# Multi-query attention, 64 sequences on one core: value products in the key-block order 0, 3, 1, 2, and the four bias heads of a partition as neighbours

## The chip, the core and the metric

The kernel runs on one core of a Trainium2 chip. A core has five engines that run their own instruction streams: TensorE (PE in the profile; PEld is its weight load), VectorE (DVE), ScalarE (ACT), GpSimd (POOL) and SyncE (SP). Here SP issues nearly all DMA transfers, one after the other, and 16 DMA engines carry them. The metric is device time in microseconds (us), the median of several executions. One more execution is taken with the hardware profiler; the profile and the trace come from it.

## The reference, cut to what matters

```python
# x: 64 x 128 x 512; 16 heads of 64, one shared key/value head; f32 throughout
xn = layernorm(x, g_in)
q = (xn @ Wq).reshape(b, n, 16, 64).transpose(0, 2, 1, 3) * 64 ** -0.5
k, v = split(xn @ Wkv)                        # 64 columns each
k, v = [null_k; k], [null_v; v]               # one null key and value in front
sim = einsum('bhid,bjd->bhij', q, k) + [null_attn_bias, attn_bias]
sim = where(causal or masked, -max, sim)
out = einsum('bhij,bjd->bhid', softmax(sim), v)
out = out.transpose(0, 2, 1, 3).reshape(b, n, 1024) @ Wo
return x + layernorm(out, g_out)
```

`attn_bias` is 16 x 128 x 128. It is the same for all 64 batches (sequences), so the kernel loads it once.

## The kernel before

**Tiles.** A batch is 128 tokens. Its scores lie in one tile `S[b]` of 128 partitions: a partition holds one query row of a quarter of the heads. The 128 partitions are four groups ("quads") of Q = 32, and a quad holds the same 32 query places for NE = 4 heads. Query rows are cut in four blocks of 32, and since the attention is causal, block i needs only its first (i + 1) x 32 keys. So a partition's row holds for each of its four heads the four blocks with 32, 64, 96 and 128 keys behind each other (`BLOCK[i]`), and a null column beside each. The blocks 0 and 1 are the first half (`KEYS[0]`, 192 columns of two heads in a PSUM room), 2 and 3 the second.

**Heads.** The four heads of a partition are stored in the order (r, f): r is the half of a 128-column query block in which a head lies, f the block. A head is number 8v + 4u + 2f + r, where 2u + v is the quad. Since r is the outer index in the tile and the inner one in the head's number, `load_bias` (lines 197 to 206) makes one transfer for each u, block, v and r: 32 in all, of 32 x 2 rows each. A row has 32, 64, 96 or 128 columns of f32.

**Bias, once, at the start.** `load_second` queues on SP: the input tiles `x_4` to `x_7`, a small key load, the bias of u = 1, `nbh` (the null bias), the bias of u = 0. Behind them on SP, in this order, come the key copies of `kv_pair_out` (line 397), the mask of the first four batches (`load_mask`, line 141), the value round trip (`vd`, `vr`, lines 407 and 412), `nv2`, `x_8` and `x_9`, the second mask, and then `wo` and `gob`. A transfer's completion semaphore is one of eight that go round, so a transfer also waits until the one eight before it has landed. GpSimd cuts the loaded bias to the causal triangle (`causal`, line 214), VectorE takes the null bias off (`null_shift`, lines 230 and 235), and then `bias_add` (line 684, GpSimd) adds bias and mask into `S[b]` for each batch. The mask goes through ScalarE first (`mask_neg`, line 671, tile `mneg`). On ScalarE, `mask_neg(0)` stands in front of the copies of two query blocks (line 460) that the first scores need.

**Loop.** Two batches a, b are one turn (`turn`, `body`; the last two are written out in `turn_end`, `body_end`). A turn's scores are computed on TensorE in 64 x 64 tiles (line 731), added into `S` by VectorE (`scores_add`, lines 746 and 748), reduced to a maximum, put through exp on ScalarE (line 767), scaled on GpSimd (line 791), and transposed in 32 x 32 blocks by VectorE into `sb` (line 821). In the next turn's head, behind that turn's scores, `values` multiplies them with the values. Then comes TensorE's work for the next group's queries (lines 367, 516, 582, 648) and for the output projection (line 953). Every engine takes its instructions in the order written; the order is set by hand.

**Value products.** `values(b)` (lines 860 to 881) runs over the key blocks j = 0 to 3. Key block j is seen by the query blocks i = j to 3, so its product has (4 - j) x 32 query columns for each of two heads: 256, 192, 128 and 64 columns. Each j is one wave of 8 matmuls on 8 array tiles (four quads s in the rows, two head halves r in the columns), each with its own weights, 32 values x 64. Wave j = 0 writes all of the PSUM room, the others add to the part they see. A matmul in f32 shows in the trace as two passes, each with its own weight load.

Of the kernel before, what the change touches and what calls it, by code (L numbers as in the profile page):

```python
# [17 lines left out]
def kernel(  # L18
# [59 lines left out]
    nc = tc.nc  # L78
    B, N, DIM = x.shape
    H = attn_bias.shape[0]  # L80
    DH = w_kv.shape[1] // 2
# [8 lines left out]
    Q = 32  # L90
    NQ = P // Q
    NF = NC // 2
    R8 = 2 * NF
    NE = H // NQ
    NF2 = NF // 2
    KEYS_OF = tuple((i + 1) * Q for i in range(NQ))
# [3 lines left out]
    BLOCK = tuple(slice(K_AT[i], K_AT[i] + KEYS_OF[i]) for i in range(NQ))  # L100
    KEYS = slice(1, LOW - 1), slice(LOW + 1, ROW - 1)
# [49 lines left out]
    nbp = const.tile([P, NE], FP, name="nbp")  # L151
    nv2 = const.tile([P, 1], FP, name="nv2")
    nbh = const.tile([P, H], FP, name="nbh")
    biasp = const.tile([P, NE, ROW], FP, name="biasp")
# [26 lines left out]
    def load_second():  # L181
        for m in range(4, 8):
            load_x(m)
        nc.sync.dma_start(
            out=nkv, in_=cond[0:2].rearrange("r d -> (r d)").unsqueeze(1)
        )
        load_bias(1)
        nc.sync.dma_start(out=nbh, in_=null_bias.partition_broadcast(P))
        load_bias(0)
# [5 lines left out]
            )  # L195

    def load_bias(u):
        bias_r = attn_bias.rearrange("(v u f r) i j -> u v r i f j", v=2, u=2, r=2)[u]
        for i in (3, 2, 1, 0):
            for v in range(2):  # L200
                quad = slice((2 * u + v) * Q, (2 * u + v + 1) * Q)
                for r in range(2):
                    nc.sync.dma_start(  # L203
                        out=biasp[quad, r * NF2 : (r + 1) * NF2, BLOCK[i]],
                        in_=bias_r[v, r, i * Q : (i + 1) * Q, :, 0 : KEYS_OF[i]],
                    )

    def causal(u):

# [13 lines left out]

    def null_shift(u):

        rows = slice(u * DH, (u + 1) * DH)
        for v in range(2):
            quad = slice((2 * u + v) * Q, (2 * u + v + 1) * Q)
            first = v * R8 + u * NE
            nc.vector.tensor_copy(  # L230
                nbp[quad].rearrange("p (r f) -> p r f", r=2),
                nbh[quad, first : first + NE].rearrange("p (f r) -> p r f", r=2),
            )
        for keys in KEYS:
            nc.vector.tensor_tensor(
                biasp[rows, :, keys],
                biasp[rows, :, keys],
                nbp[rows].unsqueeze(2).broadcast_to([DH, NE, keys.stop - keys.start]),
                ALU.subtract,
            )  # L240
# [425 lines left out]
    S, nmax, rsum = {}, {}, {}  # L666
# [72 lines left out]
    pss = {}  # L739

    def scores_add(b, hf):
        sv = S[b][:, :, KEYS[hf]].rearrange("p (r f) j -> p r f j", r=2)
        pv = pss.pop((b, hf))
        if isinstance(pv, list):
            for r in (1, 0):
                nc.vector.tensor_tensor(sv[:, r], pv[r], sv[:, r], ALU.add)
        else:
            nc.vector.tensor_tensor(sv, pv, sv, ALU.add)
# [111 lines left out]
    def values(b):  # L860

        g, t = divmod(b, GB)
        sb = sbs.pop(b)
        for j in range(NQ):
            slots = slice(j * (1 + SLOT), j + SLOT * SLOT + 1, SLOT)
            for s in range(NQ):
                quad = slice(s * Q, (s + 1) * Q)
                for r in range(2):
                    nc.tensor.matmul(  # L869
                        pos[b][s][r * DH : (r + 1) * DH, :, j * Q :].rearrange(  # L870
                            "p f (i q) -> p f i q", q=Q
                        ),
                        vr[g][quad, t, j, :],
                        sb[quad, slots, r * NF2 : (r + 1) * NF2, :].rearrange(
                            "p i f q -> p f i q"
                        ),
                        start=(j == 0),
                        stop=True,
                        skip_group_check=(j > 0),
                        tile_position=(s * Q, r * DH),  # L880
                    )
# [159 lines left out]
    def turn(d):  # L1041

        a, b, p = 2 * d, 2 * d + 1, 2 * d - 2
        g = d // 2 + 1
        homes = (ps_y, "Y"), (ps_q, "a")
        if d == 1:
            homes = homes[::-1]
        scores(a, 0, (homes[0], (ps_w, "w")))
        scores(b, 0, (homes[1], (ps_w, "w")))
        scores(a, 1)  # L1050
        scores(b, 1, ((ps_y, "X"), (ps_q, "c")))
        scores_add(a, 0)
        scores_add(b, 0)
        scores_max(a, 0)
        scores_add(a, 1)
        scores_add(b, 1)
        po = values_rooms(p)
        values(p)
        values(p + 1)
        if d % 2 and (d + 1) // 2 < NG:  # L1060
            mask_neg((d + 1) // 2)
        bias_add(a + 2)
        if d % 2 == 0:
            token_sum(g, 1)
            token_sum(g, 2)
        exps(a, 0)
        values_out(p, po)

    def turn_end(d):

        a, b, p = 2 * d, 2 * d + 1, 2 * d - 2
        if d == PAIRS:
            blocks_T(late_T.pop(), (4,))
            late_nmr(p - 3)
            late_norm(p - 3)
            late_gain(p - 4)
            late_residual(p - 4, nc.gpsimd)
            values_rooms_apart(p)
            result_room(p)
            for m in (p, p + 1):  # L1080
                values(m)
                values_out_one(m)
            return
# [538 lines left out]
    norm_apply(6)  # L1622
    norm_T(4)
    null_shift(1)
    causal(0)
    q_batches((5,))
# [3 lines left out]
    q_batches((6,))  # L1630
    norm_T(6)
    null_shift(0)
    bias_add(0, (slice(0, LOW), slice(LOW, ROW)))
    q_half(7, 0)
# [105 lines left out]
```

## Time and profile before

| | us |
|---|---|
| median of 3 executions | 1033.31 |
| lowest, highest | 1033.29, 1035.83 |
| the profiled execution | 1035.0 |
| its span, first to last instruction | 1033.2 |
| TensorE busy in it | 1016.9 |

The mean granted clock of TensorE over the span is 0.995 of full speed. In the profile a row of a timeline or of the chain begins with its start and its length in us; "L203" is line 203 of the kernel; `x16` is a count; `[6.01 <-ACT qT L460]` is the time that the engine stood idle before, and what ended it. A row of a group ends with its busy time, the mean length of one in ns, and the idle time before. SPq, ACTq and PEq stand for what an engine's sequencer does, issuing transfers above all. Lengths of matmuls are modelled by the profiler, and a matmul's record lasts beyond its last column, so that matmuls behind each other overlap.

### The profile page before, as it was taken

The page shows a single profiled execution, that of the slowest core. Times are in us where ns is not written, and L with a number is a line of the kernel's source. Part 1 is how long each engine was busy: PE and PEld are TensorE (multiplying, and loading weights), DVE is VectorE, ACT ScalarE, POOL GpSimd, SP SyncE. Part 2 cuts the span into 40 slices and gives each one's busy share as a digit, 9 for nine tenths or more (in the row PEclk, how much of TensorE's full clock was granted, in tenths as well). Part 3 has the DMA queues.
Part 4 walks back from the last instruction along what each step waited for, and adds up shares of the span by engine and source line. Part 5 has one row for each costly group of instructions (what it writes and reads, how often), then busy time and mean ns, then how long its engine had stood idle before and what let it go on. Part 6 is the DMA issues. An engine that isn't in the chain of part 4 may idle for free.

```text
span 1033.2 us, 32182 instructions
## 1 busy us (share of the span) xinstructions
PE 1016.9 (98%) x12493; PEld 903.5 (87%) x12493; DVE 809.8 (78%) x2216; ACT 666.1 (64%) x2705; POOL 736.1 (71%) x768
## 2 busy tenths in 40 slices
PE   9799999999999999999999999999999999999997
PEld 9688888888888888888888888888888888888886
DVE  6476777787888788888787887787888787877687
ACT  4565786656766566775656866567765657755583
POOL 3687758677696676868668596776867768586676
PEclk9899999999999999999999999999999999999999
DMA  6504214152240524314142250513315142131221
GB/s 194 151 27 125 95 68 122 58 149 85 97 125 32 157 71 133 107 47 136 60 148 92 78 137 33 168 66 114 115 38 153 63 146 94 68 101 36 67 84 63
DMA packets 68017, 100.79 MB, mean 98 GB/s; under 512 B 24852, under 2 KB 30232, under 8 KB 66072
## 3 DMA queue, kind: packets, MB, share of 16 engines
q1 hardware_dynamic: 67568, 98.34, 30.8%
q8 instruction: 98, 1.61, 0.6%
q14 instruction: 55, 0.45, 0.1%
q10 hardware_dynamic: 296, 0.40, 0.1%
HBM read 63.06 MB, written 33.55 MB: 94 GB/s over the span
## 4 chain that ended last, share of the span: by engine, by line
PE 95%; DMA 2%; SPq 1%; POOL 1%; issue 1%; ACT 0%; POOLq 0%; DVE 0%; DVEq 0%
PE pyX L953 19%; PE pa L516 15%; PE pyY L953 10%; PE pc L516 10%; PE po L869 8%; PE pkv L367 6%; PE pyw L953 5%; PE pl L582 4%; PE pm L648 4%; PE ps L731 3%; PE sc_X L731 2%; PE sc_Y L731 2%; PE pq L451 1%; PE py_s L953 1%; PE sc_a L731 1%; SPq L203 1%
## 5 line engine op out<-in xcount | busy, mean ns | idle before, releaser
L767 ACT ACTIVATE s<-s,nmax 128x33 f32<-128x33 f32 (+3 forms) x1024 | 357.9, 354 | 30.5 <-DVE nmax L754 30.5
L791 POOL TENSOR_TENSOR s<-s,rinv 128x128 f32<-128x128 f32 (+3 forms) x256 | 181.7, 732 | 117.8 <-DVE rinv L785 117.7
L684 POOL TENSOR_TENSOR s<-biasp,mneg 128x1296 f32<-128x1296 f32 (+1 forms) x65 | 188.3, 2899 | 85.9 <-ACT mneg L671 58.5
L767 ACT ACTIVATION_READ_ACCUMULATOR s<-s,nmax 128x1 f32 x1024 | 196.1, 191 | 0.0
L981 ACT COPY y<-pyX 128x256 f32<-128x256 f32 x29 | 10.8, 372 | 167.8 <-PE pyX L953 155.2
L754 DVE TENSOR_REDUCE nmax<-s 128x4 f32<-128x132 f32 (+3 forms) x256 | 112.5, 482 | 0.1
L953 PE MATMUL pyX<-wT,oT 128*128 128x256 f32 x464 | 109.7, 379 | 0.0
L953 PE MATMUL pyX<-wo,oT 128*128 128x256 f32 x464 | 109.7, 379 | 0.0
L821 DVE STREAM_TRANSPOSE sb<-s 128x256 f32<-128x256 f32 (+3 forms) x194 | 103.9, 587 | 0.6 <-POOL s L791 0.5
L953 PEld LDWEIGHTS pyX<-wo,oT 128*128 128x128 f32 x464 | 86.0, 190 | 10.5
L528 ACT COPY ku<-pa 128x256 f32<-128x256 f32 x118 | 43.3, 367 | 76.5 <-issue 58.0
L869 PE MATMUL po<-sb,vr 32*64 32x256 f32 (+1 forms) x4064 | 90.3, 304 | 2.1 <-issue 2.0
L953 PEld LDWEIGHTS pyX<-wT,oT 128*128 128x128 f32 x464 | 84.0, 190 | 9.2
L869 PEld LDWEIGHTS po<-sb,vr 32*64 32x64 f32 x4064 | 79.5, 130 | 14.1 <-issue 11.5
L537 DVE TENSOR_TENSOR qT<-pc,ku 128x256 f32<-128x256 f32 x118 | 48.8, 413 | 49.4 <-ACT ku L528 25.1
L892 ACT ACTIVATE oT<-po,nv 128x512 f32<-128x512 f32 (+1 forms) x127 | 74.6, 669 | 19.4 <-PE po L869 19.4
L933 POOL TENSOR_TENSOR oT<-oT 128x512 f32<-128x512 f32 x64 | 80.6, 1277 | 4.5 <-PE pyw L953 2.2
L288 POOL TENSOR_TENSOR rstd<-rstd,nhalf 128x1 f32<-128x1 f32 x64 | 35.2, 556 | 57.5 <-DVE rstd L287 52.8
L516 PE MATMUL pa<-xS,wq 128*128 128x256 f32 x264 | 67.8, 379 | 0.0
L598 DVE TENSOR_TENSOR qT<-pl,kp 128x128 f32<-128x128 f32 x112 | 32.1, 286 | 42.7 <-PE pl L582 41.7
L367 PE MATMUL pkv<-xT,wkv 128*128 128x256 f32 x256 | 63.3, 391 | 0.4 <-issue 0.4
L516 PE MATMUL pa<-xT,wq 128*128 128x256 f32 x236 | 60.6, 379 | 0.0
(208 smaller groups left out, 2555.9 us busy)
## 6 DMA issues: line engine op xcount, KB each, us to landing
res<-in_x_dram SPq DMA_DIRECT2D x64, 256.0 KB
out_dram<-y SPq DMA_DIRECT2D x63, 256.0 KB
x<-in_x_dram SPq DMA_DIRECT2D x62, 256.0 KB
xd<-xb SPq DMA_DIRECT2D x14, 1024.0 KB
xT<-xd SPq DMA_DIRECT2D x56, 256.0 KB
vr<-vd SPq DMA_DIRECT2D x64, 128.0 KB
kT<-kT SPq DMA_DIRECT2D x32, 64.0 KB
vd<-vb SPq DMA_DIRECT2D x32, 64.0 KB
```

The source lines that it names most:

```text
L367: nc.tensor.matmul(pkv, wkv[:, kc, :], xT[g][:, t : t + 2, kc, :], start=(kc == 0), stop=(kc == KC - 1),)
L516: nc.tensor.matmul(prod[tag], w[:, kc, f * P : (f + 1) * P], t[:, :, kc, :], start=(start and kc == 0), stop=(kc == HK - 1), skip_group_ch ...
L684: nc.gpsimd.tensor_tensor(S[b][:, :, keys], biasp[:, :, keys], mneg[:, t, keys] .unsqueeze(1) .broadcast_to([P, NE, keys.stop - keys.start ...
L731: nc.tensor.matmul(home[r][u * DH : (u + 1) * DH, f, keys], qT[g, u * NF2 + f, t // 2][rows, t % 2, i], kT[rows, t, 0 : KEYS_OF[i]], start ...
L754: nc.vector.tensor_reduce(nmax[b][:, hf, k * NE : (k + 1) * NE], S[b][:, :, WITH_NULL[i]], AX.X, ALU.max, negate=True,)
L767: nc.scalar.activation(row, row, AF.Exp, bias=nmax[b][:, hf, k : k + 1], accum_out=rsum[b][:, hf, k : k + 1],)
L791: nc.gpsimd.tensor_tensor(sv, sv, rinvs[b, hf][:, k : k + NE] .unsqueeze(2) .broadcast_to([P, NE, KEYS_OF[i]]), ALU.mult,)
L821: nc.vector.transpose(sbs[b][:, at : at + n].rearrange("p j e q -> p e j q"), S[b][:, :, keys].rearrange("p e (j k) -> p e j k", k=Q),)
L869: nc.tensor.matmul(pos[b][s][r * DH : (r + 1) * DH, :, j * Q :].rearrange("p f (i q) -> p f i q", q=Q), vr[g][quad, t, j, :], sb[quad, slo ...
L892: nc.scalar.activation(to, src, AF.Identity, bias=nv2)
L933: eng.tensor_tensor(o, a, b, op)
L953: nc.tensor.matmul(prod[key], h[:, c, :], w[:, c, :], start=(start and c == 0), stop=(c == HC - 1), skip_group_check=not start,)
```

## The change

The four heads of a partition are stored in the order of their numbers, e = 2f + r. `load_bias` then takes the four neighbours in one transfer: 16 transfers of 32 x 4 rows, in the same order of u, block and v. Three places follow: the null bias is copied without a reordering; `scores_add` reads `S` with r inside f; a value product takes every second head of `sb` (`r::2`) instead of two neighbours. Apart from that, `values` takes its key blocks in the order 0, 3, 1, 2, so the waves have 256, 64, 192 and 128 columns.

```diff
     def load_bias(u):
-        bias_r = attn_bias.rearrange("(v u f r) i j -> u v r i f j", v=2, u=2, r=2)[u]
+        bias_r = attn_bias.rearrange("(v u e) i j -> u v i e j", v=2, u=2)[u]
         for i in (3, 2, 1, 0):
             for v in range(2):
                 quad = slice((2 * u + v) * Q, (2 * u + v + 1) * Q)
-                for r in range(2):
-                    nc.sync.dma_start(
-                        out=biasp[quad, r * NF2 : (r + 1) * NF2, BLOCK[i]],
-                        in_=bias_r[v, r, i * Q : (i + 1) * Q, :, 0 : KEYS_OF[i]],
-                    )
+                nc.sync.dma_start(
+                    out=biasp[quad, :, BLOCK[i]],
+                    in_=bias_r[v, i * Q : (i + 1) * Q, :, 0 : KEYS_OF[i]],
+                )
...
     def null_shift(u):
...
-            nc.vector.tensor_copy(
-                nbp[quad].rearrange("p (r f) -> p r f", r=2),
-                nbh[quad, first : first + NE].rearrange("p (f r) -> p r f", r=2),
-            )
+            nc.vector.tensor_copy(nbp[quad], nbh[quad, first : first + NE])
...
     def scores_add(b, hf):
-        sv = S[b][:, :, KEYS[hf]].rearrange("p (r f) j -> p r f j", r=2)
+        sv = S[b][:, :, KEYS[hf]].rearrange("p (f r) j -> p r f j", r=2)
...
     def values(b):
...
-        for j in range(NQ):
+        for j in (0, 3, 1, 2):
...
-                        sb[quad, slots, r * NF2 : (r + 1) * NF2, :].rearrange(
+                        sb[quad, slots, r::2, :].rearrange(
```

More of the change, by code (lines that the diff above doesn't have):

```diff
@@ L224, in null_shift @@
     def null_shift(u):
-        rows = slice(u * DH, (u + 1) * DH)
         for v in range(2):
@@ L229, in null_shift @@
             first = v * R8 + u * NE
-            nc.vector.tensor_copy(
-                nbp[quad].rearrange("p (r f) -> p r f", r=2),
-                nbh[quad, first : first + NE].rearrange("p (f r) -> p r f", r=2),
-            )
+            nc.vector.tensor_copy(nbp[quad], nbh[quad, first : first + NE])
+        rows = slice(u * DH, (u + 1) * DH)
         for keys in KEYS:
```

## The prediction

> **What bounds the kernel now.** I read the page first: busy time by engine, then the chain of waits.
>
> ```profile
> span 1033.2 us, 32182 instructions
> PE 1016.9 (98%) x12493; PEld 903.5 (87%) x12493; DVE 809.8 (78%) x2216; ACT 666.1 (64%) x2705; POOL 736.1 (71%) x768
> PE 95%; DMA 2%; SPq 1%; POOL 1%; issue 1%; ACT 0%; POOLq 0%; DVE 0%; DVEq 0%
> ```
>
> TensorE is busy for 98% and is 95% of the chain: in the loop nothing else sets the pace. An edit on another engine is worth something only where TensorE stands still; an edit to TensorE's own work counts once per turn of the loop. The change has one of each kind. So the second view was the table of stretches with the granted clock (PEclk), to see where TensorE stands still.
>
> ```profile
> 29.50:36.00 6.50, 0.49 (x5) 0.38 (x4) 1.70 (x2) 2.48 (x6) 3.96 (x10) 0.81 0.38 85
> 36.00:44.70 8.70, 8.64 (x143) 7.12 (x142) 4.32 (x10) 5.34 (x27) 8.39 (x6) 0.75 0.52 140
> 72.00:1027.00 955.00, 951.90 (x11907) 845.39 (x11895) 762.21 (x2105) 629.06 (x2584) 692.11 (x710) 1.00 0.31 95
> ```
>
> (Columns after the stretch: its length, then busy time of PE, PEld, DVE, ACT and POOL, then clock, DMA share, GB/s.) Of the 16.3 us without a matmul, 6.0 lie in one hole, from 29.5 to 36 us, and right behind it the clock is below 1: 0.81 and 0.75 in these two stretches, 1.00 in the loop. The chain of waits, in order of time, says what the hole waits for.
>
> ```profile
> 16.45 0.89 SPq L203
> ...
> 28.66 0.42 SPq L203
> 29.19 0.54 SPq L397
> 29.83 0.53 SPq L397
> 30.41 3.09 DMA m<-in_mask_BxS_bk_dram
> 33.52 1.92 ACT mneg L671 x4
> 35.44 0.25 ACT qT L460
> ```
>
> SP issues bias transfers back to back (L203), then two key copies (L397), then the mask (L141). The mask lands 3.1 us after its issue; ScalarE makes `mneg` of it (L671), and queued behind that on ScalarE is the copy of a query block (L460) for which the first scores wait. The hole is SP's issue time, passed on through the mask.
>
> The third view is the timeline of one clean turn's value products (L869), which are TensorE's own work.
>
> ```profile
> 385.11 2.62 PE L869 MATMUL po<-sb,vr 32*64 32x256 f32 x128
> 387.67 0.70 PE L367 MATMUL pkv<-xT,wkv 128*128 128x256 f32 x2
> 390.74 1.73 PE pyX L953 x8
> PEld po L869 <- issue: 11.5, 46, 0.8
> ```
>
> Two batches are 128 matmuls (64 value products of two passes each, since a product in f32 shows as two), and the next work starts 387.67 - 385.11 = 2.56 us after them. Eight array tiles work side by side, so each streams 2 x 2 x (256 + 192 + 128 + 64) = 2560 columns; at 1.73/8 = 0.216 us for 256 columns (last-but-one row, from the chain) that is 2.16 us. So 0.40 us of a clean turn is not streaming. The last row says that in some turns the weight loads also wait for nothing the profile shows, 11.5 us in all; that goes on, since the number of TensorE instructions stays.
>
> **The change part by part.**
>
> *Sixteen bias transfers instead of 32.* Bytes, row lengths and rows stay; a transfer now has 32 x 4 = 128 rows instead of 64. What it takes SP to issue:
>
> ```profile
> 1.18 1.84 SPq L164 DMA_DIRECT2D wq<-in_L_cond_Wq_dram  x4
> 4.80 0.43 SPq L178 DMA_DIRECT2D wkv<-in_L_cond_Wkv_dram  x1
> 9.18 11.91 SPq L203 DMA_DIRECT2D biasp<-in_fside_16xSxS_dram  x16
> 21.14 0.43 SPq L188 DMA_DIRECT2D nbh<-cond_null_attn_bias_dram  x1
> 21.61 7.48 SPq L203 DMA_DIRECT2D biasp<-in_fside_16xSxS_dram  x16
> ```
>
> The second group of 16 takes 7.48/16 = 0.47 us each. Four weight transfers of 128 rows of 2 KB take 1.84/4 = 0.46 each, and one of 512 rows 0.43: the price is per transfer, not per row, and I take 0.47. The first eight of the first group are stretched by waits for earlier loads (11.91 us for 16); they stay where they are, the eighth issued at 16.45 and done at 17.34, but they now hold all of the first half of the bias. Then `nbh` goes out at 17.4 instead of 21.1, the second eight run from 17.9 to 21.6 instead of 21.6 to 29.1: 7.5 us earlier. Everything behind them on SP moves with them: both key copies, the mask, `vd`, `vr`, `nv2`, `x_8`, `x_9`, the second mask, `wo`, `gob`.
>
> The key copies need the keys, and the hole has neighbours:
>
> ```profile
> 20.98 0.47 ACT L391 ACTIVATE kT<-pkv,nkv 64x256 f32<-64x256 f32 x1
> 25.70 0.57 ACT L321 COPY xT<-pxT 128x512 f32<-128x512 f32 x1
> 28.91 0.60 PE L320 MATMUL pxT<-wR,x 128*128 128x128 f32 x4
> 35.75 0.42 PE L731 MATMUL sc_Y<-kT,qT 64*64 64x32 f32 x2 [6.01 <-ACT qT L460]
> 38.84 4.46 PE L451 MATMUL pq<-xT,wq 128*128 128x256 f32 x16
> 43.23 0.25 PE L731 MATMUL sc_X<-kT,qT 64*64 64x32 f32 x2
> 44.63 10.63 PE L451 MATMUL pq<-xT,wq 128*128 128x256 f32 x48
> ```
>
> Keys are ready at 21.45, so the copies go at 21.7 and 22.3, the mask at 22.9, and it lands at 26.0. ScalarE is busy until 26.27 with the copy before `mneg`, so `mneg` runs 26.3 to 28.2, the query copy to 28.5, and the next two copies to 29.4. TensorE reaches the scores at 29.4 and has almost no hole: I leave 0.2 of the 6.0 us, a gain of 5.8. With the hole goes the low clock behind it. The first scores took 38.84 - 35.75 = 3.1 us, the next ones, at full clock, 44.63 - 43.23 = 1.4: 1.7 gained. The 16 projections took 43.23 - 38.84 = 4.4; the 48 after them run at 10.6/3 = 3.5 for 16: 0.9 gained. Together 5.8 + 1.7 + 0.9 = **8.4 us**.
>
> Late next would be the bias itself:
>
> ```profile
> 29.53 2.53 POOL L214 TENSOR_SCALAR_AFFINE_SELECT biasp<-biasp 32x128 f32<-32x128 f32 x8 [5.58 <-DMA biasp<-in_fside_16xSxS_dram]
> 32.09 1.08 DVE L235 TENSOR_TENSOR biasp<-biasp,nbp 64x896 f32<-64x896 f32 x1 [0.20 <-POOL biasp L214]
> 34.47 8.93 POOL L684 TENSOR_TENSOR s<-biasp,mneg 128x392 f32<-128x392 f32 x4 [2.41 <-ACT mneg L671]
> 37.55 0.36 DVE L746 TENSOR_TENSOR s<-sc_w,s 128x192 f32<-128x192 f32 x1 [4.38 <-PE sc_w L731]
> ```
>
> The cut now ends at 32.06, 3.4 us behind the last issue at 28.66, and the null shift at 33.2, 4.5 behind it; behind a last issue at 21.1 that is 24.5 and 25.6, both before `mneg` (28.2); GpSimd's four additions start when `mneg` is half done, at 27.3 instead of 34.5, and the first scores are added near 30.5 instead of 37.5. These engines move 7.2 us where TensorE moves 8.4; the 1.2 us is covered, since ScalarE waits 1.69 us for a projection at 41.6 in the trace of before:
>
> ```profile
> 41.61 0.37 ACT L460 COPY qT<-pq 128x256 f32<-128x256 f32 x1 [1.69 <-PE pq L451]
> ```
>
> Bounds of this term: if the 1.2 us isn't covered, 7.2 is left; if a transfer of 128 rows takes SP twice as long, 0.94, then eight of these stand for the 24 bias issues now behind the eighth, and 24 x 0.47 - 8 x 0.94 = 3.8 is left. Above, 9: the whole hole, 6.0, and 3 us of clock.
>
> [...]
>
> *The order 0, 3, 1, 2.* Work and instruction count stay. Where are the 0.40 us of a turn? Matmuls grouped by shape, in three stretches of the clean turn (385.3 to 386.1, 386.1 to 386.45, then to 387.72):
>
> ```profile
> L869 PE MATMUL po<-sb,vr 32*64 32x192 f32 x16 | 0.5, 321 | 0.0
> L869 PE MATMUL po<-sb,vr 32*64 32x128 f32 x16 | 0.4, 268 | 0.0
> L869 PE MATMUL po<-sb,vr 32*64 32x256 f32 x8 | 0.6, 420 | 0.0
> L869 PE MATMUL po<-sb,vr 32*64 32x64 f32 x16 | 0.4, 233 | 0.0
> L869 PE MATMUL po<-sb,vr 32*64 32x64 f32 x22 | 0.8, 220 | 0.0
> ```
>
> 64 columns cost 321 - 268 = 53 ns, so 256 should last 374: the eight that follow the short (64-column) wave last 420 and waited some 46 ns inside for weights; the short ones themselves are longer at the first batch's end (233) than at the second's (220), behind which no wave comes. So the loss sits around the short wave. My reading, an assumption: about two waves fit ahead, so that a wave's weights enter only when a matmul two waves back has ended. A matmul ends 268 - 107 = 0.16 us after its stream; add 0.05 for the load (the 46 ns) and 0.03 for handing over: the wave between must cover 0.24 us. Two passes cover 0.43, 0.32, 0.22, 0.11 for 256, 192, 128, 64 columns. So the short wave leaves 0.13 open if something follows it, the 128 wave 0.02. Now, the short wave is last in a batch: in the first batch of a turn it is open, in the second the turn ends. Per turn 0.13 + 2 x 0.02 = 0.17. With the change it stands between 256 and 192 in both batches, and 128 is open once: 0.26 + 0.02 = 0.28. That is 0.11 us **dearer** per turn, over 4096/128 = 32 turns 3.5 us; I take 3.0, since in turns where the loads wait anyway some of it hides. Bounds from the row below: cheapest, all of the 0.40 but the first load (131 ns) goes, -0.27 x 32 = -8.6; dearest, the array runs empty behind each short wave, 0.16 + 0.13 + 0.03 = 0.32 twice a turn in place of the 0.17, +0.47 x 32 = +15.
>
> ```profile
> L869 PEld LDWEIGHTS po<-sb,vr x4064: 127/131/133, 71.8 to 1014.2; 32*64 32x64 f32 x194
> ```
>
> [...]
>
> *Heads as neighbours.* `scores_add` reads and writes the same elements at other strides (0.36 us in the row of L746), the null copy keeps its 32x4, the moving rows of a value product keep runs of 32 columns. Nothing: VectorE is 78% busy and TensorE covers it; were these additions a tenth slower, VectorE would still be under 85%.
>
> Sum: -8.4 + 3.0 = -5.4. The profiled execution took 1035.0 us (span 1033.2 and 1.8 around it): 1029.6. The median, 1033.31, is 1.7 below that execution, so on its scale 1027.9; I say 1028.
>
> **Rivals.**
>
> *The order costs nothing or gains* (the 64 wave is spread out, the load queue is deeper than I assume). For it: 0.40 us of a turn isn't streaming. Against: the waits sit at the short wave, which now stands inside both batches. 1033.3 - 8.4 = 1024.9; with half of the 8.6, 1020.6.
>
> *Only half of the start is won*, because issuing goes by rows and not by transfers, so that the sixteen don't do what they say: 3.8 us of hole gone, 2.2 left, and the clock as it falls. For it: no bias transfer of 128 rows is in the trace. Against: 0.46 and 0.43 us for transfers of 128 and 512 rows. 1033.3 - 3.8 + 3.0 = 1032.5; with the low clock avoided, 2.6 less.
>
> *Slower: the array runs empty behind the short wave.* Its place is the turn from 64 to 192 columns, in both batches of every turn; if no load is ready there, each costs 0.32 us, and the term is the dear bound, +15: 1033.3 - 8.4 + 15 = 1039.9. For it: 46 ns of waiting at the one such place today. Against: that place costs some 0.13 and not 0.32. It decides from 8.4/32 = 0.26 us more per turn.
>
> **How the numbers follow.** Forecast 0.52 (1026 to 1030.5), order free or gaining 0.27, half the start 0.13, slower 0.08. The range leaves out the slower case and the far end of the gain: 1021 to 1032.5. A measurement can tell 0.3% (3.1 us) from no change: below 1030.2 lie the first two cases, but for a little of the first's upper end, 0.76; within, that end and most of the half start, 0.17; above 1036.4 most of the slower case, 0.07.
>
> **What would show it.** Right: 16 rows of L203, the mask issued near 23 us, no hole above 0.5 us at the first scores, clock 1.00 from 29.5 to 44.7, first value product near 63.4 instead of 71.8, and clean turns of value products of 2.67 us instead of 2.56. Wrong: a bias transfer over 0.8 us; a new hole at the second scores or at the projections after them; clean turns at 2.45 us or less (the order gains) or above 2.83 (it eats the start's gain).

## The result and the profile after

| | before, us | after, us |
|---|---|---|
| median of 5 executions | 1035.74 | 1029.19 |
| lowest, highest | 1033.29, 1035.85 | 1027.39, 1031.3 |
| ratio after to before | | 0.9945, 95% interval 0.9925 to 0.9965 |
| span of the profiled execution | 1033.2 | 1026.7 |

The change is 0.55% faster, 0.35 to 0.75% by the interval. (The ratios compare all executions of both kernels, so they need not equal the ratio of the two medians.) Timed once more beside one of the experiments (below), it gave 1030.47 against 1035.13, ratio 0.9950 (0.9937 to 0.9964).

First SP's timeline in the changed kernel: start, length, line, transfer, count.

```profile
9.99 8.33 SPq L202 DMA_DIRECT2D biasp<-in_fside_16xSxS_dram  x8
18.37 0.43 SPq L188 DMA_DIRECT2D nbh<-cond_null_attn_bias_dram  x1
18.84 3.76 SPq L202 DMA_DIRECT2D biasp<-in_fside_16xSxS_dram  x8
22.70 1.18 SPq L393 DMA_DIRECT2D kT<-kT  x2
23.93 0.58 SPq L141 DMA_DIRECT2D m<-in_mask_BxS_bk_dram  x1
```

The second eight take 3.76/8 = 0.47 us each, with 128 rows as with 64 before: the price is per transfer. The mask leaves at 23.9 instead of 30.4. What ScalarE and TensorE make of it, from their timelines:

```profile
27.00 1.93 ACT L667 ACTIVATE mneg<-m,neg 128x128 f32<-128x128 uint8 x4 [0.78 <-DMA m<-in_mask_BxS_bk_dram]
28.83 0.35 ACT L456 COPY qT<-pq 128x256 f32<-128x256 f32 x1
29.55 0.37 ACT L456 COPY qT<-pq 128x256 f32<-128x256 f32 x1
29.38 0.30 PE L727 MATMUL sc_Y<-kT,qT 64*64 64x32 f32 x4
31.25 3.72 PE L447 MATMUL pq<-xT,wq 128*128 128x256 f32 x16
34.90 0.25 PE L727 MATMUL sc_X<-kT,qT 64*64 64x32 f32 x2
63.45 2.73 PE L865 MATMUL po<-sb,vr 32*64 32x256 f32 x128
66.12 0.70 PE L363 MATMUL pkv<-xT,wkv 128*128 128x256 f32 x2
```

No row has the 6 us of idle time in front of it any more. The first scores start at 29.38 and end, with the wait for the second query copy among them, at 31.25; the projections after them take 3.65 us. The first value product starts at 63.45 instead of 71.78, 8.3 us earlier. In the stretches, the clock stays whole:

```profile
29.50:36.00 6.50, 6.48 (x140) 5.43 (x144) 3.86 (x9) 4.78 (x25) 6.50 (x3) 1.00 0.37 102
36.00:44.70 8.70, 8.70 (x55) 7.55 (x46) 7.48 (x11) 7.14 (x39) 8.11 (x7) 1.00 0.93 288
```

TensorE's busy time is 6.48 of 6.50 us where it was 0.49, at a clock of 1.00 where it was 0.81 and 0.75. The rest of the span grew: from the first value product to the end it was 1033.2 - 71.8 = 961.4 us and is 1026.7 - 63.5 = 963.2. So of 8.3 us won at the start, 1.8 went back in the loop: 6.5 in all, the difference of the spans.

The last two rows of the timeline above are a clean turn of value products: 66.12 - 63.45 = 2.67 us from the first product to the next work, 2.56 before. Matmuls grouped by shape, in the piece of a clean turn (314.3 to 314.9) that holds the first batch's short wave and the 192 wave behind it:

```profile
L865 PE MATMUL po<-sb,vr 32*64 32x192 f32 x15 | 0.7, 344 | 0.0
L865 PE MATMUL po<-sb,vr 32*64 32x64 f32 x16 | 0.3, 216 | 0.0
```

The waiting moved with the short wave: before, the 192-column matmuls took 321 ns and the 256-column ones that followed the short wave waited; now 192 columns follow it and take 344 on average over their two passes. The short wave's own matmuls, which lasted 233 behind a 128-column wave, last 216 behind one of 256.

### The profile page after: what moved, and what is told of

Its sections match the earlier page's. It is cut to its first block, busy times and chain, and to the rows that moved or that the text cites. A ratio compares the mean times of both kernels' runs of the same rounds, so it can differ in the third digit from the quotient of the medians.

```text
span 1026.7 us, 32158 instructions
## 1 busy us (share of the span) xinstructions
PE 1016.6 (99%) x12493; PEld 901.4 (88%) x12493; DVE 810.1 (79%) x2216; ACT 666.4 (65%) x2705; POOL 738.4 (72%) x768
## 4 chain that ended last, share of the span: by engine, by line
PE 98%; POOL 1%; issue 1%; POOLq 0%; DVE 0%; DVEq 0%
PE pyX L949 20%; PE pa L512 15%; PE pyY L949 10%; PE pc L512 10%; PE po L865 9%; PE pkv L363 6%; PE pyw L949 5%; PE pl L578 4%; PE pm L644 4%; PE pq L447 3%; PE ps L727 2%; PE sc_X L727 2%; PE sc_Y L727 2%; PE py_s L949 1%; PE sc_a L727 1%; PE sc_w L727 1%
## 5 line engine op out<-in xcount | busy, mean ns | idle before, releaser
L865 PEld LDWEIGHTS po<-sb,vr 32*64 32x64 f32 x4064 | 78.9, 131 | 13.3 <-issue 10.4
```

The source lines that it names most:

```text
L865: nc.tensor.matmul(pos[b][s][r * DH : (r + 1) * DH, :, j * Q :].rearrange("p f (i q) -> p f i q", q=Q), vr[g][quad, t, j, :], sb[quad, slo ...
```

## The experiments

Two questions were open: whether start and order really are two separate terms of the sizes given, and what makes the order dear. "Clean turn" is the shortest of the 32 turns, from the first value product to the next work; in each kernel 8 to 12 turns lie within 0.01 us of it, and the others are longer.

**1. The bias alone.** The changed kernel with one line put back:

```diff
-        for j in (0, 3, 1, 2):
+        for j in range(NQ):
```

> The changed kernel with the key blocks back in the order 0, 1, 2, 3. Theory (start and order are two separate terms): hole at the first scores at most 0.3 us, first value product near 63.5 us, clean turn of value products 2.55 us again; 8 to 9 us below the kernel before, some 1025, faster than the change. Rival (the order does not matter, or helps): clean turn 2.66 us as in the change, or the time no lower than the change's.

Measured: 1026.07 us against 1034.99, ratio 0.9918 (0.9904 to 0.9932); once more 1026.61 against 1035.13, ratio 0.9920 (0.9907 to 0.9934). TensorE's timeline of a clean turn:

```profile
782.09 2.62 PE L865 MATMUL po<-sb,vr 32*64 32x256 f32 x128
784.64 0.70 PE L363 MATMUL pkv<-xT,wkv 128*128 128x256 f32 x2
```

2.55 us, as before the change. The first value product starts at 63.05, with 63.5 expected. The start is worth 8.5 to 8.9 us by the medians, and this version beats both kernels. It also shows that the neighbouring heads cost nothing: from the first value product to the end it takes 961.3 us, the kernel before 961.4.

**2. The order alone.** The kernel before, with only the order:

```diff
-        for j in range(NQ):
+        for j in (0, 3, 1, 2):
```

> The kernel before with nothing but the key-block order 0, 3, 1, 2. Theory: hole of 6.0 us and first value product at 71.8 us as before, clean turn 2.66 us instead of 2.55, so 0.11 x 32 = 3.5 us slower than the kernel before. Rival (the order costs a clean turn something but saves other waits of the weight loads): clean turn 2.66 us, but the time within 1.5 us of the kernel before.

Measured: 1039.02 against 1034.99, ratio 1.0037 (1.0024 to 1.0050), so 3.8 us slower by the ratio and 4.0 by the medians. Timeline, at the first scores and in a clean turn, and the wait of the weight loads from the list of waits:

```profile
35.95 0.42 PE L731 MATMUL sc_Y<-kT,qT 64*64 64x32 f32 x2 [6.20 <-ACT qT L460]
700.68 2.73 PE L869 MATMUL po<-sb,vr 32*64 32x256 f32 x128
703.35 0.48 PE L367 MATMUL pkv<-xT,wkv 128*128 128x256 f32 x1
PEld po L869 <- issue: 12.2, 46, 1.0
```

The hole is there (6.2 us), and the clean turn is 2.67 us. The clean turns alone, 2.663 us against 2.551 before rounding, make 0.112 x 32 = 3.6 us, which lies inside the interval of the time (2.5 to 5.2). The rival, that the order saves other waits of the loads and leaves less than 1.5 us, falls: the time is outside it, and those waits are 12.2 us against 11.5 before. So the two terms are separate and add within what the times can tell: by the ratios -8.5 and +3.8 make -4.7, and the change has -5.7 and -5.2, with -4.7 inside both intervals.

**3 and 4. The order in one batch of the pair.** In the changed kernel, one of the two new lines in each:

```diff
-        for j in (0, 3, 1, 2):
+        for j in ((0, 1, 2, 3) if b % 2 else (0, 3, 1, 2)):    # 3: first batch
+        for j in ((0, 3, 1, 2) if b % 2 else (0, 1, 2, 3)):    # 4: second batch
```

> Only the first batch of a pair takes its blocks in the order 0, 3, 1, 2, the second in 0, 1, 2, 3. Theory A (two waves of loads fit ahead; a short wave costs 0.13 us unless it is the turn's last): one exposed short wave as in the kernel before, clean turn 2.55 to 2.58 us. Theory B (only the turn's last wave counts, a longer one makes the turn end later): 2.55. Theory C (each batch in the new order costs the same): 2.61.

> Only the second batch of a pair takes its blocks in the order 0, 3, 1, 2, the first in 0, 1, 2, 3. Theory A: two exposed short waves as in the change, clean turn 2.66 us. Theory B: 2.66. Theory C: 2.61.

Clean turns of 3, then of 4:

```profile
376.27 2.63 PE L865 MATMUL po<-sb,vr 32*64 32x256 f32 x128
378.83 0.48 PE L363 MATMUL pkv<-xT,wkv 128*128 128x256 f32 x1
```

```profile
440.03 2.73 PE L865 MATMUL po<-sb,vr 32*64 32x256 f32 x128
442.69 0.48 PE L363 MATMUL pkv<-xT,wkv 128*128 128x256 f32 x1
```

2.56 and 2.66 us (single executions took 1026.85 and 1029.94). The new order costs nothing in the first batch and all of its 0.11 in the second. Theory C, a cost per batch, falls. A and B both stand.

**5. Another last wave.**

```diff
-        for j in (0, 3, 1, 2):
+        for j in (0, 2, 3, 1):
```

> Key blocks in the order 0, 2, 3, 1, so the waves have 256, 128, 64, 192 columns and the turn ends with 192. Theory A (short wave exposed in both batches, what comes last has no weight of its own): clean turn 2.66 us, as with 256, 64, 192, 128. Theory B (the cost grows with the columns of the last wave, 0.11 us for 64 more): 2.55 + 0.22 = 2.77 us.

```profile
189.29 2.73 PE L865 MATMUL po<-sb,vr 32*64 32x256 f32 x128
191.95 0.48 PE L363 MATMUL pkv<-xT,wkv 128*128 128x256 f32 x1
```

2.66 us, not 2.77: a last wave of 192 columns costs no more than one of 128. Theory B falls. (The single execution took 1031.75 us, 1.8 more than experiment 4; the clean turn is the same, so that lies in the other turns.)

**6. Without the short wave.**

```diff
-        for j in (0, 3, 1, 2):
+        for j in (0, 1, 2):
```

> Key blocks 0, 1, 2 only; key block 3, the 64-column wave, is left out of the products of both batches, everything else as in the change. Streaming falls by 4 passes of 56 ns, 0.22 us. Theory A: the exposed short wave goes too, clean turn 2.55 - 0.34 = 2.21 us. Theory B: it ends with 128 columns, 2.55 - 0.22 + 0.11 = 2.44 us. An equal loss per wave: 2.55 - 0.22 - 0.07 = 2.26 us.

```profile
495.59 2.28 PE L865 MATMUL po<-sb,vr 32*64 32x256 f32 x96
497.80 0.48 PE L363 MATMUL pkv<-xT,wkv 128*128 128x256 f32 x1
```

2.21 us, theory A's number (the single execution took 1013.54 us). Against the old order a turn is 0.34 us shorter, and the short waves' columns are only 0.22 of that: 0.12 is the exposure that went with them.

**7. The bias in 24 transfers.** In the version of experiment 1:

```diff
-                nc.sync.dma_start(
-                    out=biasp[quad, :, BLOCK[i]],
-                    in_=bias_r[v, i * Q : (i + 1) * Q, :, 0 : KEYS_OF[i]],
-                )
+                for e in ((slice(0, NE),) if u else (slice(0, 2), slice(2, NE))):
+                    nc.sync.dma_start(
+                        out=biasp[quad, e, BLOCK[i]],
+                        in_=bias_r[v, i * Q : (i + 1) * Q, e, 0 : KEYS_OF[i]],
+                    )
```

> Order 0, 1, 2, 3, and the bias in 24 transfers: u = 1 in 8 of 128 rows, u = 0 in 16 of 64 rows. Theory (0.47 us of SP per transfer, passed on through the mask): the mask leaves 8 x 0.47 = 3.8 us later than with 16, near 27.7 us, the hole at the first scores is 3.5 us, and the time lies 3.5 us over that with 16 transfers, or up to 6 if the clock drops. Rival (issuing goes by rows or bytes): mask, hole and time as with 16 transfers.

SP's and TensorE's timelines, and the stretch behind the hole:

```profile
17.97 7.48 SPq L203 DMA_DIRECT2D biasp<-in_fside_16xSxS_dram  x16
26.77 0.58 SPq L141 DMA_DIRECT2D m<-in_mask_BxS_bk_dram  x1
32.51 0.30 PE L728 MATMUL sc_Y<-kT,qT 64*64 64x32 f32 x2 [3.03 <-ACT qT L457]
33.80:37.20 3.40, 3.40 (x40) 2.71 (x31) 3.03 (x7) 1.33 (x8) 3.40 (x2) 0.50 0.27 60
```

Measured: 1032.69 us (ten executions, 1028.42 to 1034.03), ratio 0.9965 (0.9951 to 0.9978) to the kernel before. By the ratios that is some 5 us above experiment 1, between the 3.5 and the 6 expected. Eight more transfers of 0.47 us bring back 3.0 us of hole, where 3.5 was expected, and 3.4 us at half clock; the first value product comes at 68.4 us, 5.3 later than in experiment 1. The same bytes and rows in more transfers take longer: the rival, rows or bytes, falls.

**8. The mask ahead of the second half of the bias, in the kernel before**, all 32 transfers kept:

```diff
         nc.sync.dma_start(out=nbh, in_=null_bias.partition_broadcast(P))
+        load_mask(0)
         load_bias(0)
...
     kv_pair_out(2, pkv2)
-    load_mask(0)
```

> The kernel before, all 32 transfers and the old order, but the first mask is queued ahead of the second half of the bias instead of behind the key copies. Theory (the hole is the wait for the mask, and next late are the key copies, which still leave SP at 29.2 us): the query copies no longer wait, the first scores start near 29.4, those on the copied key half wait until about 32, a hole near 2.5 us, clock kept, 5 to 6 us faster than before. Rival (the bias itself holds the start): hole of 4 us or more and at most 3 us faster.

```profile
21.69 0.43 SPq L141 DMA_DIRECT2D m<-in_mask_BxS_bk_dram  x1
29.73 1.18 SPq L398 DMA_DIRECT2D kT<-kT  x2
31.81 0.32 PE L732 MATMUL sc_w<-kT,qT 64*64 64x32 f32 x2 [2.07 <-DMA kT<-kT]
31.80:35.20 3.40, 3.39 (x62) 2.98 (x63) 2.29 (x4) 0.00 (x0) 3.32 (x4) 0.50 0.30 55
```

Measured: 1030.07 us, ratio 0.9950 (0.9932 to 0.9967), some 5 us faster, without a transfer less. So it was the mask that made the hole, and the key copies, next late as expected, hold TensorE for the 2.07 us that are left (2.5 was expected). The bias itself wasn't waited for. One thing was expected wrongly: the clock did fall, to 0.50 for 3.4 us.

**9 and 10. The change and the bias alone, side by side.** Experiment 9 is the changed kernel and 10 the kernel of experiment 1, both as they are.

> The change as it is, once more beside the kernel before and beside the version with the old order. Theory: 5 to 6 us below the kernel before, 3 to 4 us above the version with the old order. Rival (the order's cost is lost in the other waits of the weight loads): less than 1.5 us between the change and that version.

> The version with 16 transfers and the order 0, 1, 2, 3, once more, on the same chip as the change. Theory: 8 to 9 us below the kernel before and 3 to 4 us below the change. Rival: less than 1.5 us below the change.

Measured: 1030.47 and 1026.61 us, with 1035.13 for the kernel before: 4.7 and 8.5 below it, 3.9 us apart. The ranges don't touch (1028.0 to 1030.89, 1026.32 to 1027.26). The rival falls.

## Why the prediction was right

**The start.** -8.4 was forecast, and the first value product comes 8.3 us earlier. The chain held step by step: 0.47 us per transfer, the mask out early (23.9, forecast 22.9: the first bias transfer itself left 0.8 later in this execution, at 9.99 instead of 9.18), `mneg` as the mask lands (27.0, forecast 26.3), the scores at 29.4, no low clock. The total is closer than its parts, and that is luck. The scores start 35.75 - 29.38 = 6.4 us earlier, where 5.8 was set for the hole; they and the projections behind them gain 1.2 and 0.7 us, where 1.7 and 0.9 were set, since the first scores took 1.87 us instead of 1.4: the second query copy ended at 29.9 and not at 29.4. In experiment 10, where the mask leaves at 22.82 us, the first scores take the forecast 1.4 us and the first value product starts at 63.04.

Experiments 7 and 8 show the cause from both sides: more transfers with everything else kept bring the hole back, and the mask moved ahead takes most of it away with all transfers kept. That the lag of the other engines would be covered held too: GpSimd's additions start 6.5 us earlier (27.94 instead of 34.47), so the lag is 1.8 us and not 1.2, and still 8.3 us arrive at the first value product. Heads as neighbours cost nothing, as forecast (experiment 1).

**The order.** 0.11 us per turn was forecast against what the order may seem to be for, and 0.11 was measured (2.67 against 2.56, and 2.67 against 2.55 in experiments 2 and 1). What experiments 3 to 6 show is that a short wave with something behind it costs a turn some 0.12 us, and nothing as the turn's last: 2.55 to 2.58, 2.66, 2.66 and 2.21 were expected before they ran, and 2.56, 2.66, 2.66 and 2.21 measured. With the prediction's own terms, 0.13 for a short wave and 0.02 for a 128 wave, experiments 5 and 6 come to 2.68 and 2.18, so these terms hold to some 0.03 us. The 0.03 us for handing over, one of the pieces of the 0.24 us that a wave was to cover, stands in no row; only the whole was tested.

That the load waits for the end of a matmul two waves back, from which the 0.24 us and with it the 0.13 and the 0.02 follow, was an assumption, and no run shows it: how many waves fit ahead wasn't varied by itself. What the runs show in its place is the exposure, some 0.12 us for each short wave with something behind it (experiments 3 to 6). A simpler mechanism can be worked out against the same numbers: if a tile's next load, 131 ns, could only hide behind the pass that streams just then (54 ns for 64 columns, 108 for 128), the new order would cost 0.05 us per turn and experiment 6 would come to 2.08 us. Measured were 0.11 and 2.21, so it falls. An order that costs nothing, as the first rival had it, is out too: a turn costs 0.11 us more.

**The size of the order's term.** It was set to 3.0 and not 3.5, because part of it was to hide in turns whose loads wait anyway. The runs don't decide between the two: the order alone costs 3.8 us by the ratio, but the interval reaches from 2.5 to 5.2, and the change lies 3.9 us above the bias alone by the medians of experiments 9 and 10, and 3.1 by the first medians of the two (1029.19 and 1026.07). Summed over the traces, the 32 turns take 90.6 us before and 90.2 and 90.6 in experiments 1 and 10; in the new order they take 92.4 in the change, 93.6 in experiment 2 and 94.0 in experiment 9. So two traced executions differ by 1.8 to 3.8 us, and in experiments 7 and 8, old order with a hole at the start, the turns take 92.3 and 92.1. The 1.8 of the profiled pair is the low end: 32 clean turns are 3.6 us longer, but what the turns have above a clean one is 7.2 us after and 9.0 before. The list of waits points the same way:

```profile
PEld po L865 <- issue: 10.4, 44, 1.0
```

10.4 us against 11.5. These waits differ from one execution to the next (10.3 to 13.1 in the experiments), and so do the times of one kernel (1027.39 to 1031.3). Where they come from was not settled: in the list they are `issue`, time in which the loads wait for nothing that the profile shows.

**Rivals.** Order free or gaining: out by experiment 2. Half the start: out, since a transfer of 128 rows takes the 0.47 us of one of 64, and the whole hole went. Slower, the array empty behind the short wave: the exposure is some 0.12 us per short wave (experiment 6), not 0.32. As a difference of medians the sum was -5.4, and -6.6 and -4.7 were measured. The forecast time of 1028 stood on the median of three, 1033.31; with five executions that median is 1035.74, because the kernel's executions fall near 1033.3 or 1035.8. That 1029.19 still came within 1.2 us of 1028 is in part luck: the kernel before proved slower, and the gain larger, than the sum had them.

## What to carry to other kernels

Count what stands on a DMA-issuing queue ahead of the transfer that is waited for, and what the next engine has queued behind that wait: here 16 more issues of 0.47 us than needed held a 64 KB mask, the mask held a copy, and the copy held TensorE (a hole of 6.01 us) and its clock (0.81 and 0.75 in the two stretches from 29.5 to 44.7 us). For packed matmuls of unequal width like these, put a narrow wave where nothing follows; here each narrow wave with a wide one behind it was exposed, some 0.12 us a wave. And take a two-part change apart: the half that lost 3 to 4 us hid behind the half that won some 8.5.

## What was not expected of the hardware

A hole of 2.07 us in TensorE's work was followed by the half clock, where a hole near 2.5 us had been expected to leave the clock whole: in the profiled execution of experiment 8 the clock falls to 0.50 from 31.8 to 35.2 us, in experiment 7 (3.03 us) it does so for 3.4 us too, and before the change (6.01 us) for longer, 0.81 and 0.75 on average over 15 us. It was not so in every execution. At half clock for 3.4 of some 1030 us the mean clock is 0.998, and the four executions of experiment 8 have 0.998, 0.998, 1.000 and 0.999, so in two of them the clock cannot have been at half for that long. What makes the difference isn't shown; only the first one's trace was kept.

With the short wave exposed in both batches, a turn costs the same whether a 128- or a 192-column wave is its last: 2.66 us in experiments 4 and 5. The columns of a turn are the same in all orders, and of their places only what stands behind the short wave showed.
